# A graph layer with residual and layer norm: 68 copied columns per engine and octet, register loads of eight, sums in two PSUM banks, and the product of x and W1b made three and copied two octets ahead

## The chip, the core and the metric

The kernel runs on one core of a Trainium2 chip. The core has five engines with a stream of instructions each: TensorE (PE in the profile; PEld is its weight load), VectorE (DVE), ScalarE (ACT), GpSimd (POOL) and SyncE (SP), which here only issues transfers and loads registers. The metric is the device time of one execution in microseconds (us), less is better. Before the change the median of three runs is 5184.74 us (5167.56 to 5185.11).

## What is computed

There are 12500 nodes with 64 features each and 400000 edges, sorted by their target node.

```python
def _L0_gnn_ref(x, edge_index, edge_attr, W1, b1, W2, b2, W3, b3):
    src, dst = (edge_index[0], edge_index[1])
    m_in = jnp.concatenate([x[src], x[dst], edge_attr], axis=-1)
    h = jax.nn.silu(m_in @ W1 + b1)
    messages = jax.nn.silu(h @ W2 + b2)
    agg = jax.ops.segment_sum(messages, dst, num_segments=x.shape[0])
    node_in = jnp.concatenate([x, agg], axis=-1)
    return jax.nn.silu(node_in @ W3 + b3)
...
x = _layernorm(x + _L0_gnn_ref(...), axis=-1)
```

W1 has three blocks of rows: W1a for x[src] (64 rows), W1b for x[dst] (64 rows) and one for the edge attributes (16 rows).

## The kernel before

**Tiles and octets.** The edges are cut into 3125 tiles of 128. Eight tiles are an octet; 391 octets are the turns of the main loop, which is unrolled (line 601 and on). Since the edges are sorted by target, all targets of an octet lie in a window of 48 nodes.

**The first layer of an octet** (`first_layer`, line 434) has two shares. The share of the targets and the attributes is one matmul, line 441, with weights `xw`: 96 rows of x W1b for the window, twice over and masked, and 32 rows of attribute weights. The 96 rows are made for every octet: SyncE fetches the window's 48 columns of x (`window_load`, line 392), TensorE multiplies them by W1b (`window_product`, line 397) into a PSUM tile named `mm`, and VectorE copies that with the mask into one of three `xw` tiles (`window_copy`, line 402). The share of the sources comes in one of three ways, and pairs of tiles (256 edges) are handed out to them:

- GpSimd gathers rows of x W1a, made in advance, from memory: one indirect transfer per tile of 128 edges (`gather`, line 373), three octets ahead, into five buffers `ga`. TensorE turns and adds them at line 454.
- VectorE and ScalarE copy columns of x, which stays in on-chip memory transposed (`xs`), one instruction per edge, into a tile `cx` of 128 columns with two edges each (`columns`, lines 297 and 299). Where a column lies comes from a register, loaded beforehand from the list of source indices (line 290, a register load of up to 16 or 8 values). Per octet VectorE copies 32 + 32 columns and ScalarE 32 + 28 (`VCOLS`, `ACOLS`). A `cx` tile that is full takes the place of two gathers; TensorE multiplies it by W1a at line 451. The index list of a tile is fetched by SyncE (`index`, line 351) and scaled to addresses by VectorE (`address`, line 359).
- SyncE fetches 16 single rows per octet (`rows`, line 324), which makes a pair every 16 octets.

The first 12 octets (`RAW`) gather raw rows of x and multiply them by W1a themselves (lines 443 to 449), while the tables of x W1a are made (`table`, line 175).

**The rest of an octet.** ScalarE applies silu (line 458, `h`), TensorE multiplies by W2 (`second_layer`, lines 467 and 469), ScalarE applies silu again (line 473, `m`). `add_up` (line 482) sums the messages per node with 8 matmuls against a 0/1 matrix `eh`, into one quarter of a PSUM tile, `pg`, with four quarters used by turns. `add_window` (line 487) adds that to the sums of all nodes, on VectorE. VectorE makes the 0/1 matrices by comparing (`compare_dst`, line 424, and `compare_nodes`, line 430). Every four tiles of nodes that are complete get their second part (lines 499 to 552).

**The order.** TensorE, ScalarE, VectorE and SyncE run their instructions in the order in which the loop issues them (line 598); waits between engines are put in by the framework, and a tile is overwritten only when those who read its earlier content are done. In turn o the streams are:

- SyncE: index list for o+3, now and then other loads, the window of o+3, 16 rows.
- TensorE: product for o+1, first layer of o, sums of o-2, second layer of o-1.
- VectorE: add of o-4, comparison of targets for o+1, 32 columns, window copy for o+1, comparison of nodes for o+1, 32 columns, addresses for o+2.
- ScalarE: 32 columns, h of o, 28 columns, m of o-1.

**PSUM.** There are eight banks: two for `mm` (pool `mis`: products, raw tiles, tables, node products), one for `wrow`, two for `p1` (first layer), two for `p2` (second layer), one for `pg` (the sums).

Of the kernel before, what the change touches and what calls it, by code (L numbers as in the profile page):

```python
# [27 lines left out]
AHEAD = 3  # L28
RAW = 12
TABLES = 7  # L30
ACOLS = (32, 28)
VCOLS = (32, 32)
ROWS = 16
LOADS = (16, 8)
XBASE = (0, 64 << 18)
XADDR = 36864
LAG = CT * P // 32
# [60 lines left out]
def windows(ctx, tc, ident, badi, pa, x, xt, src_c, src_row, dst_c, dst_row, attr_t, dst_2, attr_2, base, w1, b1, w2, b2, w3, b3, out, edges):  # L98
# [70 lines left out]
    zero = const.tile([P, 1], F32, name="zero")  # L169
    nc.vector.memset(zero, 0.0)  # L170

    mis = ctx.enter_context(tc.tile_pool(name="mis", bufs=2, space=PSUM))


    def table(c):
        n = min(8 * P, N - c)
        ps = mis.tile([P, 8, D], F32, name="mm")
        k = (n + P - 1) // P
        for i in range(k):
            o = c + i * P  # L180
            nc.tensor.matmul(ps[:, i, :], xs[0:D, o:o + P], w1ab[:, 0, :], start=True, stop=True)
        j = c // (8 * P) % RB
        t = v[:, 2 * j:2 * j + 2].rearrange("p a i d -> p (a i) d")
        nc.scalar.copy(t[:, :k], ps[:, :k])
        f = n // P
        if f:
            nc.scalar.dma_start(pa[c:c + f * P, :].rearrange("(i p) d -> p i d", p=P), t[:, :f])
        if n % P:
            nc.scalar.dma_start(pa[c + f * P:c + n, :], t[:n % P, f, :])
# [43 lines left out]
    w1bb = fast.tile([D, 2, D], F32, name="w1bb")  # L233
    nc.vector.tensor_copy(w1bb, w1ab[:, 1:2, :].to_broadcast([D, 2, D]))
    xw = []
    for k in range(3):
        t = fast.tile([P, P], F32, name=f"xw{k}")
        nc.vector.memset(t, 0.0)
        for q in range(2):
            nc.sync.dma_start(t[E + q * A:E + (q + 1) * A, q * D:(q + 1) * D], w1[2 * D:2 * D + A, :])  # L240
        xw.append(t)
# [6 lines left out]
    with tc.tile_pool(name="gat", bufs=AHEAD + 2) as gat, tc.tile_pool(name="drp", bufs=2) as drp, \  # L248
# [2 lines left out]
            tc.tile_pool(name="work", bufs=2) as work, tc.tile_pool(name="win", bufs=3) as win, \  # L251
            tc.tile_pool(name="ps1", bufs=2, space=PSUM) as ps1, \
            tc.tile_pool(name="ps2", bufs=2, space=PSUM) as ps2, \
            tc.tile_pool(name="psa", bufs=1, space=PSUM) as psa, \
            tc.tile_pool(name="cx", bufs=4) as cx, tc.tile_pool(name="cxi", bufs=3) as cxi, \
            tc.tile_pool(name="rx", bufs=2) as rx, tc.tile_pool(name="rxi", bufs=2) as rxi, \
            tc.tile_pool(name="nx", bufs=2) as nx, tc.tile_pool(name="nv", bufs=1) as nv:
# [10 lines left out]
        cols, indices = {}, {}  # L268
        xb = xs.bitcast(U8)

        def columns(o, eng, part):
            if o < RAW:
                return
            lo = (o - RAW) * RATE
            if eng == ENG.Activation:
                lo, n = lo + sum(ACOLS[:part]), ACOLS[part]
            else:
                lo, n = lo + sum(ACOLS) + sum(VCOLS[:part]), VCOLS[part]
            hi, todo = lo + n, n
            while lo < hi:  # L280
                j, e0 = lo // (2 * P), lo % (2 * P)
                if j >= len(pairs):
                    return
                n = min(hi - lo, P - e0 % P, LOADS[lo > hi - todo])
                if pairs[j] not in cols:
                    cols[pairs[j]] = cx.tile([P, P], F32, name="cx")
                t = cols[pairs[j]].bitcast(U8)
                s = e0 // P
                h = slice(s * D, (s + 1) * D)
                _, regs = nc.values_load_multi_w_load_instructions(  # L290
                    indices[j][0:1, e0:e0 + n], engines=(eng,), min_val=XBASE[s] + XADDR,
                    max_val=XBASE[s] + XADDR + 4 * (N - 1), skip_runtime_bounds_check_because="src names a node")
                for e, r in zip(range(e0 % P, e0 % P + n), regs):
                    to, frm = t[h, 4 * e:4 * e + 4], xb[h, ds(r - (XBASE[s] + XADDR), 4)]
                    if eng == ENG.DVE:

                        nc.vector.tensor_reduce(to, frm[:, :, None], AX.X, OP.max)  # L297
                    else:
                        nc.scalar.copy(to, frm)  # L299
                lo += n  # L300


        rpairs = []
# [55 lines left out]
                    nc.vector.tensor_scalar(t[:, h], t[:, h], 4.0, float(XBASE[s] + XADDR), op0=OP.mult, op1=OP.add)  # L359

        winrow, winreg = {}, {}
        sums = psa.tile([P, 4, S], F32, name="pg")

        def gather(o):
            c, t0, n, first, last = octs[o]
# [29 lines left out]
        def window_product(o):  # L395
            pw = mis.tile([P, P], F32, name="mm")
            nc.tensor.matmul(pw[:E, :], winrow[o].rearrange("k s w -> k (s w)"), w1bb.rearrange("k s m -> k (s m)"),  # L397
                             start=True, stop=True)
            winrow[o] = pw

        def window_copy(o):
            nc.vector.tensor_tensor(xw[o % 3][:E, :], winrow.pop(o)[:E, :], mask[:E, :], op=OP.mult)  # L402

        def load(c, o0=0, o1=CT // OT):

# [28 lines left out]
        def first_layer(o):  # L434
            c, t0, n, first, last = octs[o]
            n2 = n + n % 2
            k = n2 // 2
            ga = got.pop(o)
            oh, eh = hots.pop(o)
            p1 = ps1.tile([P, OT // 2, P], F32, name="p1")  # L440
            nc.tensor.matmul(p1[:, :k], xw[o % 3], oh, start=True, stop=False, skip_group_check=True)  # L441
            if o < RAW:
                pt = mis.tile([P, OT // 2, P], F32, name="mm")
                for i in range(k):
                    nc.tensor.matmul(pt[:, i, :], ga[:, 2 * i:2 * i + 2, :].rearrange("p s d -> p (s d)"), ident,  # L445
                                     start=True, stop=True)
                xg = work.tile([P, OT // 2, P], F32, name="m")
                nc.vector.tensor_copy(xg[:, :k], pt[:, :k])
                nc.tensor.matmul(p1[:, :k], w1d, xg[:, :k], start=False, stop=True, skip_group_check=True)
            if o in pairs:  # L450
                nc.tensor.matmul(p1[:, 0, :], w1d, cols.pop(o), start=False, stop=False, skip_group_check=True)  # L451
            for i in range(1 if o in pairs else 0, k if o >= RAW else 0):
                g2 = single.pop(o) if o in rpairs and i == 1 else ga[:, 2 * i:2 * i + 2, :]
                nc.tensor.matmul(p1[:, i, :], g2.rearrange("p s d -> p (s d)"), ident,  # L454
                                 start=False, stop=(i == k - 1), skip_group_check=True)
            columns(o, ENG.Activation, 0)
            h = work.tile([P, OT // 2, P], F32, name="h")
            nc.scalar.activation(h[:, :k], p1[:, :k], AF.Silu, bias=b1s)  # L458
            made[o] = h, eh
# [16 lines left out]
        def add_up(o):  # L476
            c, t0, n, first, last = octs[o]
            m, eh = made.pop(o)
            pg = sums[:, o % 4, :]
            for i in range(n):  # L480
                s = i % 2
                nc.tensor.matmul(pg[s * D:(s + 1) * D, :], m[:, i, :], eh[:, i, :],  # L482
                                 start=(i < 2), stop=(i >= n - 2), skip_group_check=True)

        def add_window(o):
            a = agg[:, ds(winreg.pop((ENG.DVE, o)), S)]
            nc.vector.tensor_tensor(a, a, sums[:, o % 4, :], op=OP.add)  # L487


        groups = [(c, min(G * P, N - c)) for c in range(0, N, G * P)]  # L490
# [16 lines left out]
        def node_product(q):  # L507
            c, n = groups[q]
            p = n // G
            assert p * G == n  # L510
            po = mis.tile([P, G, D], F32, name="mm")
            av = agg[:, c:c + n].rearrange("k (p i) -> k i p", i=G)
            xv = xs[0:D, c:c + n].rearrange("k (p i) -> k i p", i=G)
            nc.tensor.matmul(po[:p], ones[:, :p], b3r, start=True, stop=False, skip_group_check=True)
            for i in range(G):
                nc.tensor.matmul(po[:p, i, :], xv[:, i], w3x, start=False, stop=False, skip_group_check=True)  # L516
                nc.tensor.matmul(po[:p, i, :], av[:, i], w3s, start=False, stop=(i == G - 1), skip_group_check=True)  # L517
            nodes[q].append(po)
# [62 lines left out]

        for o in range(min(AHEAD, NO)):
            gather(o)
        window_load(0)
        window_product(0)
        window_copy(0)
        load(0, 0, 1)
        load(0, 1, 3)
        window_load(1)
        window_load(2)  # L590
        relative(0, CT)
        lims = nv.tile([P, 2, LP], F32, name="lims")
        tables = list(range(0, N, 8 * P))
# [4 lines left out]
        with tc.manual_schedule(engines={ENG.PE, ENG.Activation, ENG.DVE, ENG.SP}):  # L598
            compare_dst(0)
            compare_nodes(0)  # L600
            for o in range(NO + 1):
# [27 lines left out]
                    gather(o + AHEAD)  # L629
                if o + 2 < NO and octs[o + 2][3] and o + 2:  # L630
                    load(octs[o + 2][0])
                if o + 3 < NO:
                    window_load(o + 3)
                if o + 1 < NO:
                    window_product(o + 1)
                if o % 4 == 2:
                    bases(ENG.DVE, o - 2)
                if o >= 4:
                    add_window(o - 4)
                if o + 1 < NO:  # L640
                    compare_dst(o + 1)
                columns(o, ENG.DVE, 0)
# [1 line left out]
                    first_layer(o)  # L644
                if o == 0:
                    nc.vector.tensor_copy(b2r, b2p[:, None, :].to_broadcast([3, OT, D]))
                if o + 1 < NO:
                    window_copy(o + 1)
                    compare_nodes(o + 1)
                columns(o, ENG.DVE, 1)  # L650
                if o == 1:
# [12 lines left out]
                    add_up(o - 2)  # L664
                if o >= 1:
                    second_layer(o - 1)
                address(o + 2)
                raddress(o + 2)
                rows(o)
# [21 lines left out]
        nc.vector.tensor_copy(badi, bs)  # L691

        add_up(NO - 1)
        for o in range(NO - 3, NO):
            add_window(o)
        for f, a in todo.get(NO, []):
            f(*a)
# [267 lines left out]
```

## Time and profile before

| what | value |
|---|---|
| median of three runs | 5184.74 us |
| the profiled execution | 5200.1 us |
| its span, first to last instruction | 5197.9 us |
| instructions | 107486 |
| granted clock of TensorE | 0.629 |
| gathers from the table on GpSimd (line 373) | 2619, of 0.944 us each |
| row fetches on SyncE (line 324) | 5888 |
| register loads of line 290 on VectorE | 2391, of 0.340 to 1.340 us |
| register loads of line 290 on ScalarE | 2352, of 0.305 to 1.255 us |
| line 424 and line 430 on VectorE | 0.674 and 0.545 us each |
| line 458 and line 473 on ScalarE | 0.684 and 0.593 us each |

The profile is one execution, recorded by the hardware. In its rows "DVE cx L297" is a group of instructions of VectorE at line 297 that write the tile cx; "busy" is time in which at least one of them ran, the mean is that of a single one, and "idle before" is the time in which the engine ran nothing just before them, with what ended it. "Issue" there stands for time in which the engine waited for nothing that the profile shows. Register loads, branches and the issue of transfers do not count as busy. The views in order of time give the start, the length, the engine and the line, and merge neighbours of one kind (x8: eight of them).

### The profile page before, as it was taken

What the parts mean: (1) busy time and instruction counts of PE and PEld (TensorE: products, weight loads), DVE (VectorE), ACT (ScalarE), POOL (GpSimd) and SP (SyncE); (2) the same over time, 40 slices, a digit from 0 to 9 for tenths busy, and PEclk for the clock granted to TensorE, in tenths of its full rate; (3) what the DMA queues carried; (4) which work ended last, traced back from release to release, by engine and by line L of the source; (5) the groups of instructions that cost most, each with busy time, mean ns of one, the idle gap of its engine ahead of it and who ended that gap; (6) DMA issues with size and microseconds to landing.
All of it is one profiled execution on the core that took longest, in us unless ns stands there. A gap on an engine that the chain in (4) does not pass through costs nothing. (4 is left out here: it accounts for less than half of the span.)

```text
span 5197.9 us, 107486 instructions
## 1 busy us (share of the span) xinstructions
PE 2932.5 (56%) x15131; PEld 2075.4 (40%) x15131; DVE 2641.3 (51%) x26395; ACT 2906.1 (56%) x23402; POOL 2565.3 (49%) x2724
## 2 busy tenths in 40 slices
PE   5655655555555555555564655656555555555566
PEld 3443434434433344343343434434433343344344
DVE  1255555545555555555555555555555555555555
ACT  1255555555555655655556565555556555655555
POOL 5544454454444544445444444545454444555453
PEclk7666565666666666666656566565656666665656
DMA  4321111211211121122112211211211221121121
GB/s 85 86 46 39 40 39 40 47 39 40 46 42 43 40 46 40 40 43 42 41 40 49 43 40 42 44 39 40 47 40 40 44 47 40 40 47 39 40 46 40
DMA packets 203943, 229.98 MB, mean 44 GB/s; under 512 B 133612, under 2 KB 141988, under 8 KB 202324
## 3 DMA queue, kind: packets, MB, share of 16 engines
q1 hardware_dynamic: 101528, 122.61, 10.5%
q0 software_dynamic: 86880, 89.14, 9.1%
q10 hardware_dynamic: 14812, 11.26, 0.9%
q14 instruction: 595, 4.87, 0.3%
q8 instruction: 128, 2.10, 0.2%
HBM read 216.36 MB, written 6.40 MB: 43 GB/s over the span
## 5 line engine op out<-in xcount | busy, mean ns | idle before, releaser
L373 POOL DMA_INDIRECT ga<-pa,sc x2619 | 2472.2, 944 | 2516.1 <-PE p L454 1699.8
L299 ACT COPY cx<-xs 64x4 uint8 x22560 | 2404.2, 188 | 1406.1 <-issue 1362.4
L297 DVE TENSOR_REDUCE cx<-xs 64x4 uint8 x24032 | 1910.3, 150 | 1806.6 <-issue 1740.9
L441 PE MATMUL p<-oh,xw 128*128 128x512 f32 (+1 forms) x782 | 772.4, 1089 | 1529.3 <-DVE xw L402 727.6
L441 PEld LDWEIGHTS p<-oh,xw 128*128 128x128 f32 x782 | 187.1, 297 | 1637.1 <-DVE xw L402 776.3
L482 PE MATMUL pg<-eh,m 128*64 128x48 f32 x6250 | 363.0, 277 | 588.6 <-ACT m L473 174.1
L454 PEld LDWEIGHTS p<-ident,ga 128*128 128x128 f32 x2620 | 591.3, 314 | 194.9 <-issue 193.6
L469 PE MATMUL p<-w2d,h 128*128 128x128 f32 x3126 | 642.0, 369 | 1.5 <-issue 1.4
L469 PEld LDWEIGHTS p<-w2d,h 128*128 128x128 f32 x3126 | 545.3, 263 | 133.0 <-issue 133.0
L454 PE MATMUL p<-ident,ga 128*128 128x128 f32 x2620 | 593.2, 397 | 0.0
L482 PEld LDWEIGHTS pg<-eh,m 128*64 128x64 f32 x6250 | 312.1, 189 | 680.2 <-issue 342.2
L473 ACT ACTIVATE m<-p 128x512 f32<-128x512 f32 x391 | 231.8, 593 | 474.9 <-remote 308.9
L458 ACT ACTIVATE h<-p,b1s 128x512 f32<-128x512 f32 x391 | 267.4, 684 | 319.0 <-remote 138.6
L402 DVE TENSOR_TENSOR xw<-mm,mask 96x128 f32<-96x128 f32 x391 | 110.4, 282 | 439.9 <-issue 392.4
L397 PE MATMUL mm<-w1bb,xr 64*96 64x128 f32 x782 | 241.0, 401 | 72.6 <-ACT z L523 49.9
L424 DVE TENSOR_TENSOR oh<-dr,wrow 96x512 f32<-96x512 int32 x391 | 263.6, 674 | 6.3 <-issue 3.5
L430 DVE TENSOR_TENSOR eh<-wrow,dc 128x384 f32<-128x384 f32 x391 | 213.2, 545 | 42.2 <-issue 42.2
L467 PE MATMUL p<-b2r,one 3*128 3x512 bf16 x391 | 194.5, 498 | 0.0
L451 PEld LDWEIGHTS p<-cx,w1d 128*128 128x128 f32 x364 | 116.0, 319 | 175.4 <-issue 175.4
L397 PEld LDWEIGHTS mm<-w1bb,xr 64*96 64x96 f32 x782 | 127.8, 214 | 144.7 <-issue 68.7
L487 DVE TENSOR_TENSOR agg<-agg,pg 128x48 f32 x391 | 77.3, 198 | 123.4 <-remote 32.3
L373 POOL DMA_INDIRECT ga<-in_x,sc x96 | 91.0, 948 | 63.5 <-PE mm L445 28.9
(81 smaller groups left out, 802.7 us busy)
## 6 DMA issues: line engine op xcount, KB each, us to landing
rx<-pa SPq DMA_DIRECT2D x5888, 0.2 KB
dr<-in_dst SPq DMA_DIRECT2D x260, 288.0 KB
ga<-pa,sc POOLq DMA_INDIRECT x2619
oh<-in_attr SPq DMA_DIRECT2D x130, 192.0 KB
xr<-in_xt SPq DMA_DIRECT2D x391, 24.0 KB
xs<-in_xt ACTq DMA_DIRECT2D x12, 512.0 KB
pa<-v ACTq DMA_DIRECT2D x12, 256.0 KB
xa<-in_x SPq DMA_DIRECT2D x24, 128.0 KB
```

Of the source, the lines that this page charges most:

```text
L297: nc.vector.tensor_reduce(to, frm[:, :, None], AX.X, OP.max)
L299: nc.scalar.copy(to, frm)
L373: nc.gpsimd.indirect_dma_start(out=ga[:, i, :], out_offset=None, in_=x if o < RAW else pa[:, :], in_offset=bass.IndirectOffsetOnAxis(ap=sc ...
L397: nc.tensor.matmul(pw[:E, :], winrow[o].rearrange("k s w -> k (s w)"), w1bb.rearrange("k s m -> k (s m)"), start=True, stop=True)
L424: nc.vector.tensor_tensor(oh[:E, :], dr[:, e:e + w], wn[:E, o:o + 1].to_broadcast([E, w]), op=OP.is_equal)
L430: nc.vector.tensor_tensor(eh[:, :n], row[:, None, :].to_broadcast([P, n, S]), rel[:, t0:t0 + n, None].to_broadcast([P, n, S]), op=OP.is_equal)
L441: nc.tensor.matmul(p1[:, :k], xw[o % 3], oh, start=True, stop=False, skip_group_check=True)
L454: nc.tensor.matmul(p1[:, i, :], g2.rearrange("p s d -> p (s d)"), ident, start=False, stop=(i == k - 1), skip_group_check=True)
L458: nc.scalar.activation(h[:, :k], p1[:, :k], AF.Silu, bias=b1s)
L469: nc.tensor.matmul(p2[:, 2 * i:2 * i + 2, :].rearrange("p s d -> p (s d)"), h[:, i, :], w2d, start=False, stop=(i == k - 1), skip_group_ch ...
L473: nc.scalar.activation(m[:, :n2], p2[:, :n2], AF.Silu)
L482: nc.tensor.matmul(pg[s * D:(s + 1) * D, :], m[:, i, :], eh[:, i, :], start=(i < 2), stop=(i >= n - 2), skip_group_check=True)
```

## The change

- `ACOLS` goes from (32, 28) to (36, 32) and `VCOLS` from (32, 32) to (36, 32): 68 columns per octet on each of the two engines, 136 in all where there were 124.
- `LOADS` goes from (16, 8) to 8: a part of columns was loaded as sixteen registers first and eights after; now in eights only. `columns` is split into `pieces`, `addresses` and itself; its instructions are otherwise the same.
- `pg`: instead of one tile with four quarters in one bank, a tile of its own for each octet, in two banks by turns. The add of a window comes three octets after, not four.
- `mm` gets one bank instead of two. Tables and node products use `p2`, the raw tiles of the first 12 octets use `p1`.
- Four `xw` tiles instead of three. In turn o the window of o+4 is fetched (before: o+3), the product is made for o+3 and at the end of TensorE's turn (before: o+1, at its beginning), and VectorE copies that of o+2 (before: o+1), at the same place in its turn.
- VectorE's registers for the windows (line 382) are loaded one turn earlier of every four.

```diff
-ACOLS = (32, 28)
-VCOLS = (32, 32)
+ACOLS = (36, 32)
+VCOLS = (36, 32)
 ROWS = 16
-LOADS = (16, 8)
+LOADS = 8
...
-    mis = ctx.enter_context(tc.tile_pool(name="mis", bufs=2, space=PSUM))
+    mis = ctx.enter_context(tc.tile_pool(name="mis", bufs=1, space=PSUM))
...
-        ps = mis.tile([P, 8, D], F32, name="mm")
+        ps = ps2.tile([P, OT, D], F32, name="p2")
...
-    for k in range(3):
+    for k in range(4):
         t = fast.tile([P, P], F32, name=f"xw{k}")
...
-            tc.tile_pool(name="psa", bufs=1, space=PSUM) as psa, \
+            tc.tile_pool(name="psa", bufs=2, space=PSUM) as psa, \
...
-                n = min(hi - lo, P - e0 % P, LOADS[lo > hi - todo])
+                n = min(hi - lo, P - e0 % P, LOADS)
+                yield j, e0, n
+                lo += n
...
+        def addresses(eng, j, e0, n):
+            s = e0 // P
+            _, regs = nc.values_load_multi_w_load_instructions(
+                indices[j][0:1, e0:e0 + n], engines=(eng,), min_val=XBASE[s] + XADDR,
+                max_val=XBASE[s] + XADDR + 4 * (N - 1), skip_runtime_bounds_check_because="src names a node")
+            return regs
+
+        def columns(o, eng, part):
+            for j, e0, n in pieces(o, eng, part):
+                regs = addresses(eng, j, e0, n)
...
-        sums = psa.tile([P, 4, S], F32, name="pg")
+        sums = {}
...
-            nc.vector.tensor_tensor(xw[o % 3][:E, :], winrow.pop(o)[:E, :], mask[:E, :], op=OP.mult)
+            nc.vector.tensor_tensor(xw[o % 4][:E, :], winrow.pop(o)[:E, :], mask[:E, :], op=OP.mult)
...
-                pt = mis.tile([P, OT // 2, P], F32, name="mm")
+                pt = ps1.tile([P, OT // 2, P], F32, name="p1")
...
-            pg = sums[:, o % 4, :]
+            pg = sums[o] = psa.tile([P, S], F32, name="pg")
...
-            nc.vector.tensor_tensor(a, a, sums[:, o % 4, :], op=OP.add)
+            nc.vector.tensor_tensor(a, a, sums.pop(o), op=OP.add)
...
-            po = mis.tile([P, G, D], F32, name="mm")
+            po = ps2.tile([P, OT, D], F32, name="p2")[:, :G]
...
-                if o + 3 < NO:
-                    window_load(o + 3)
-                if o + 1 < NO:
-                    window_product(o + 1)
-                if o % 4 == 2:
-                    bases(ENG.DVE, o - 2)
-                if o >= 4:
-                    add_window(o - 4)
+                if o + 4 < NO:
+                    window_load(o + 4)
+                if o % 4 == 1:
+                    bases(ENG.DVE, o - 1)
+                if o >= 3:
+                    add_window(o - 3)
...
+                if o + 2 < NO:
+                    window_copy(o + 2)
                 if o + 1 < NO:
-                    window_copy(o + 1)
                     compare_nodes(o + 1)
...
                     second_layer(o - 1)
+                if o + 3 < NO:
+                    window_product(o + 3)
```

Ahead of the loop four windows are fetched, three products made and two copied (before: three, one and one); after it, two adds are left instead of three.

More of the change, by code (lines that the diff above doesn't have):

```diff
@@ L269, in windows, with pieces @@
         xb = xs.bitcast(U8)
-        def columns(o, eng, part):
+        def pieces(o, eng, part):
             if o < RAW:
@@ L278, in columns @@
                 lo, n = lo + sum(ACOLS) + sum(VCOLS[:part]), VCOLS[part]
-            hi, todo = lo + n, n
+            hi = lo + n
             while lo < hi:
@@ L289, in columns @@
                 h = slice(s * D, (s + 1) * D)
-                _, regs = nc.values_load_multi_w_load_instructions(
-                    indices[j][0:1, e0:e0 + n], engines=(eng,), min_val=XBASE[s] + XADDR,
-                    max_val=XBASE[s] + XADDR + 4 * (N - 1), skip_runtime_bounds_check_because="src names a node")
                 for e, r in zip(range(e0 % P, e0 % P + n), regs):
@@ L299, in columns @@
                         nc.scalar.copy(to, frm)
-                lo += n
         rpairs = []
@@ L440, in first_layer @@
             p1 = ps1.tile([P, OT // 2, P], F32, name="p1")
-            nc.tensor.matmul(p1[:, :k], xw[o % 3], oh, start=True, stop=False, skip_group_check=True)
+            nc.tensor.matmul(p1[:, :k], xw[o % 4], oh, start=True, stop=False, skip_group_check=True)
             if o < RAW:
-                pt = mis.tile([P, OT // 2, P], F32, name="mm")
+                pt = ps1.tile([P, OT // 2, P], F32, name="p1")
                 for i in range(k):
@@ L583, in windows @@
             gather(o)
-        window_load(0)
-        window_product(0)
-        window_copy(0)
+        for o in range(4):
+            window_load(o)
+        for o in range(2):
+            window_product(o)
+            window_copy(o)
+        window_product(2)
         load(0, 0, 1)
         load(0, 1, 3)
-        window_load(1)
-        window_load(2)
         relative(0, CT)
@@ L693, in windows @@
         add_up(NO - 1)
-        for o in range(NO - 3, NO):
+        for o in range(NO - 2, NO):
             add_window(o)
```

## The prediction

> **What bounds the kernel now.** I read the busy times first, then the groups, then single octets in order of time, and last the waits. An octet is one turn of the main loop; 391 of them fill the 5197.9 us span, and from the 30th to the 380th the period is 13.19 us (distance between the add of one window, line 487, and the next).
>
> ```profile
> PE 2932.5 (56%) x15131; PEld 2075.4 (40%) x15131; DVE 2641.3 (51%) x26395; ACT 2906.1 (56%) x23402; POOL 2565.3 (49%) x2724
> ...
> L299 ACT COPY cx<-xs 64x4 uint8 x22560 | 2404.2, 188 | 1406.1 <-issue 1362.4
> L297 DVE TENSOR_REDUCE cx<-xs 64x4 uint8 x24032 | 1910.3, 150 | 1806.6 <-issue 1740.9
> ```
>
> No engine looks full: all stand near half. But the idle time of the two engines that copy columns is nearly all "issue", which is no wait for another engine's result. VectorE's stream in order of time shows what it is:
>
> ```profile
> 2610.69 0.62 DVE L297 TENSOR_REDUCE cx<-xs 64x4 uint8 x8 [0.30 <-issue]
> 2611.35 0.21 DVE L487 TENSOR_TENSOR agg<-agg,pg 128x48 f32 x1
> 2611.47 0.68 DVE L424 TENSOR_TENSOR oh<-dr,wrow 96x512 f32<-96x512 int32 x1
> 2612.36 1.78 DVE L297 TENSOR_REDUCE cx<-xs 64x4 uint8 x24 [0.21 <-issue]
> ...
> 2616.02 0.40 DVE L297 TENSOR_REDUCE cx<-xs 64x4 uint8 x5 [0.24 <-issue]
> 2616.70 0.21 DVE L297 TENSOR_REDUCE cx<-xs 64x4 uint8 x2 [0.28 <-issue]
> 2617.44 0.15 DVE L297 TENSOR_REDUCE cx<-xs 64x4 uint8 x1 [0.53 <-issue]
> 2618.16 0.15 DVE L297 TENSOR_REDUCE cx<-xs 64x4 uint8 x1 [0.57 <-issue]
> ```
>
> Columns start 0.0635 us apart (five in 0.40 us, one of them 0.15), until a register load (line 290) steps in: the x8 group follows a gap of 0.30 us. From 2616.7 on something else rules: one column per 0.71 us. SyncE's row fetches (line 324) are held at the same time:
>
> ```profile
> 2609.80 1.19 SPq L324 DMA_DIRECT2D rx<-pa  x4
> ...
> 2614.90 10.13 SPq L324 DMA_DIRECT2D rx<-pa  x14
> ```
>
> Four in 1.19 us before, fourteen in 10.13 us here. I call these held stretches. They lie where GpSimd's gathers are in flight while SyncE issues rows; ScalarE's columns are held too:
>
> ```profile
> 2608.50:2611.00 2.50, 2.50 (x7) 1.47 (x7) 2.18 (x30) 2.48 (x23) 0.00 (x0) 0.50 0.00 1
> 2616.50:2623.50 7.00, 3.78 (x10) 2.46 (x10) 1.38 (x11) 1.04 (x6) 4.56 (x5) 0.68 0.16 30
> ```
>
> (Stages; after the length, busy time and count of PE, PEld, DVE, ACT, POOL.) Without gathers VectorE ran 30 instructions in 2.5 us; beside five gathers, 11 in 7 us. Marking every gap of 0.5 to 1.7 us between SyncE's row instructions as held, from 300 to 5100 us, gives 2216 us of 4800 (46%). Outside them VectorE was busy 1935 of 2584 us, had a register load running in 414 more, and stood with neither for only 235. ScalarE: busy 2112, neither 334. TensorE: neither 645.
>
> Last, the waits around line 402, the copy of x W1b, and line 482, the sums:
>
> ```profile
> L402 DVE TENSOR_TENSOR xw<-mm,mask x391: 269/287/289, 13.7 to 5166.9; 96x128 f32<-96x128 f32 x196
> ...
>   PE mm L397: 3.8, 3
> ...
>   PEld p L441: 776.3, 161
> ```
>
> ```profile
> L482 PE MATMUL pg<-eh,m x6250: 222/307/343, 97.2 to 5179.0; 128*64 128x48 f32 x196
> ...
>   DVE agg L487: 168.1, 110
> ```
>
> VectorE waited 3.8 us in all for the product; TensorE waits for VectorE, at line 441 and, with line 482, for the window's add. So **the pace is VectorE's own stream plus the held stretches**, ScalarE close behind; TensorE, and GpSimd, which waits 1699.8 us for TensorE to free its buffers, follow.
>
> A check on that reading: over stretches of six octets I fitted the period to the gathers and to VectorE's extra work in them (node statistics, divisions, address arithmetic). A gather goes with 0.78 us (error 0.09), a microsecond of extra VectorE work with 0.53 us (0.13), of extra ScalarE work with 0.5 (0.4).
>
> **The change part by part.**
>
> *Columns on VectorE.* 64 become 68 per octet. Applying the slicing to all octets: 24032 become 25444, +1412 at 0.0635 us = +90 us.
>
> *Loads of eight on VectorE.* The two parts were sliced 16+8+8, now 8+8+8+8+4 and 8+8+8+8; with the cuts at tile borders 2391 loads become 3368. An eight-register load between columns sets them 0.47 us apart (0.30 idle; median of 763 spacings 0.47) where 0.06 is normal: price 0.40. There are 765 more of these: +306. A four-register load makes a spacing of 0.22 (106 cases): 0.16 each, 214 more: +34. The first load of a part runs beside the compare ahead of it (0.68 and 0.54 us) and sticks out when it has sixteen registers (1.10 us): by 0.21 and 0.24 in the rows above. With eight (0.597 us) it is covered: 682 times 0.22 = -150. That saving is 0 at least, and 0.50 each at most (1.10 - 0.597), -344; I take the rows' own gap. Seventeen more index tiles bring two address operations each of 0.2 us: +7. Sum +287 us, between 93 and 437.
>
> Some of it falls into held stretches, where the pace is set otherwise: 17% of the columns started there. 83% of 287 is 238 (77 to 363).
>
> A rule speaks more sharply against the loads: the Trainium skill, "DMA: Bandwidth & Descriptors", section on latency and other measured facts, gives register loads from memory a floor of about 600 ns. By it the 977 more loads would cost an estimated 586 us whatever their size. The trace disagrees on the floor (340 ns for four registers).
>
> *Columns on ScalarE.* 60 become 68, +2940 at 0.0935 us (32 in 3.09 us in one unbroken row) = +275 us. Its eight-register loads take 0.547 us while eight columns take 0.75, and its columns run on through them (68 of some 1200 broke the rhythm); so the finer loads cost nothing. If that cover went, the extra load time (1506 to 1762 us) would be +256. ScalarE's 334 free microseconds (362 over the span) take most of the 275; what comes through, I count below.
>
> *Gathers.* Pairs of tiles served by columns go from 182 to 199, so 34 gathers fewer. At 0.78 us each, -27 us; at GpSimd's own spacing of 1.25 us, -43; at least 0.
>
> *Product three ahead, copy two ahead, four xw.* No instruction is added per octet: product, window fetch and copy keep their counts and move by an octet. On TensorE the product is now last of its turn, behind the second layer. With one "mm" buffer instead of two, the product for o+3 must wait for line 402's copy for o+2, and line 441 of the next octet is queued behind it, then adding up, second layer and ScalarE's h. So line 441 still starts after that copy, now 0.74 us later (the two matmuls of line 397). 195 of 391 octets start line 441 within 0.4 us of the copy: 144 us at most if TensorE set the end. I take 0: it hides behind TensorE's 645 free microseconds, and nothing VectorE waits for came out of TensorE late (half of its copies start 16 us after their product). SyncE's window fetch one octet earlier moves past nothing: row fetches and index loads keep their order behind it; its buffer is freed by a product which TensorE now ends at the same place in its stream.
>
> *Sums in two banks.* The 168.1 us that line 482 waited for line 487 go; what is late next is ScalarE's m (446.9 us in the same view). On VectorE the add moves one octet closer to its sum. The sum it now needs followed m by some 1.1 us, and m(o-3) ended 7 to 18 us before the octet began. Worth 0; at best those 168, at worst the 123.4 us that line 487 has idle before it now, once more.
>
> *Node and table products in p2, the raw tiles in p1.* The 49.9 us that line 397 waited for the node sigmoid go, TensorE's again: 0. The first twelve octets take two p1 buffers each: at worst the 101.1 us of idle time ahead of line 448's twelve copies doubles; I take 0, since the tables no longer share a buffer with them.
>
> **Sum.** VectorE's path in full: +238 - 27 = +211 us. The fit gives nearly the same another way: 0.53 of 287 and 0.3 of 275 (between 0 and the fitted 0.5), less 27: +208. The profiled execution took 5200.1 us (2.2 us around its span), 15 above the median of 5184.74, so **5395 us** for the median. Its own range, from the bounds 77 to 363 of VectorE and 27 for the gathers, is 5235 to 5520.
>
> **Rivals.**
>
> *Held stretches shrink.* TensorE ends its turn earlier where line 482 waited, frees GpSimd's buffers sooner, and gathers slide into the 4.4 us per octet in which SyncE issues no rows (1.93 from the last row to the window fetch, 2.47 from there to the next row). VectorE is busy 26% of a held stretch, so each held microsecond saved gives 0.74. The stretches fill about 2400 us of the span; a fifth less gives -355 us: 5040. It beats the added work from 12% on. For it: the overlap is a matter of phase, and octets differ by 2.5 us in it (one standard deviation). Against: line 441 still hangs on the copy, rows are as many, gathers 1% fewer.
>
> *Held stretches grow.* VectorE falls behind SyncE, whose rows then come earlier into the gathers: octets in which SyncE's window fetch came before VectorE's turn began were held 7.3 to 8.4 us, those where it came 3 us after, 4.0. A tenth more is +178 us: 5573. Against: SyncE has hardly any free time to run ahead.
>
> *Nothing comes through.* VectorE's 235 idle microseconds outside (255 over the span) absorb the 238, and the gathers' 27 remain: 5185 - 27 + 15 = about 5175. Against: a passed share of 0.53 in the fit. That the columns don't move at all can't be: the lists set them.
>
> **How the numbers follow.** Forecast 55%, growth 14%, nothing 10%, shrinking 21%. Within 0.5% (5159 to 5211), which is about what this kernel's runs can tell from no change, lie 7 in 100; faster 21, the shrinking; the rest, 72, slower. Leaving out the far half of the shrinking and of the growth, 8 times in 10 the time lies in 5130 to 5560.
>
> **What would show it.** Right: some 3370 loads at line 290's successor on VectorE, an 8-column rhythm with 0.30 us gaps, the gaps after lines 424 and 430 gone, period near 13.7 us, held share still 44 to 48%, VectorE hardly waiting for TensorE. ScalarE's free time should nearly vanish, line 441's wait for the copy stay as a wait of line 397. Wrong: a held share that moves by more than 4 points, a period below 13.2, or VectorE idle for a sum or a product.

## The result and the profile after

The median after is 5481.01 us (5470.35 to 5491.54, four runs) against 5184.92 us for the kernel before beside it (5167.56 to 5191.62, four runs): a ratio of 1.0576, 95% interval 1.0543 to 1.0609. The change makes the kernel slower by 296 us; the forecast was 211 us slower.

Line numbers have moved: columns are 307 (VectorE) and 309 (ScalarE), the comparisons 433 and 439, the window copy 411, the product 406, gathers 382, row fetches 333, sums 491, the add of a window 496. First the busy times and the groups of the page after, as shown of before:

```profile
PE 2888.0 (53%) x15131; PEld 2033.1 (37%) x15131; DVE 2793.3 (51%) x27842; ACT 3226.0 (59%) x26342; POOL 2532.0 (46%) x2690
...
L382 POOL DMA_INDIRECT ga<-pa,sc x2585 | 2439.1, 944 | 2836.2 <-PE p L463 2034.4
L309 ACT COPY cx<-xs 64x4 uint8 x25500 | 2734.7, 188 | 1540.5 <-issue 1493.6
L307 DVE TENSOR_REDUCE cx<-xs 64x4 uint8 x25444 | 2073.3, 148 | 1886.7 <-issue 1801.0
L406 PE MATMUL mm<-w1bb,xr 64*96 64x128 f32 x782 | 277.5, 455 | 2050.0 <-DVE xw L411 1278.5
```

The counts are those that the working used: 25444 columns on VectorE (+1412), 25500 on ScalarE (+2940), 34 gathers fewer. TensorE did not get slower and was not asked for more; GpSimd stands idle 320 us longer (2836.2 for 2516.1), since its waits for TensorE to free its buffers grew by 335 (2034.4 for 1699.8). Those two follow. The wait for the window copy, which was line 441's (727.6 of the 1529.3 us that TensorE's matmuls stood idle before it), is now line 406's (1278.5 of 2050.0).

VectorE in order of time, some 24 us of the kernel after (start, length, engine and line, count, idle time before):

```profile
3010.97 0.67 DVE L433 TENSOR_TENSOR oh<-dr,wrow 96x512 f32<-96x512 int32 x1
3011.66 0.62 DVE L307 TENSOR_REDUCE cx<-xs 64x4 uint8 x8
3012.57 0.62 DVE L307 TENSOR_REDUCE cx<-xs 64x4 uint8 x8 [0.30 <-issue]
3013.49 0.62 DVE L307 TENSOR_REDUCE cx<-xs 64x4 uint8 x8 [0.30 <-issue]
...
3028.41 0.15 DVE L307 TENSOR_REDUCE cx<-xs 64x4 uint8 x1 [0.57 <-issue]
3029.12 0.15 DVE L307 TENSOR_REDUCE cx<-xs 64x4 uint8 x1 [0.56 <-issue]
3029.83 0.21 DVE L307 TENSOR_REDUCE cx<-xs 64x4 uint8 x2 [0.56 <-issue]
```

The gap behind the comparison of line 433 is gone, and columns come in eights with 0.30 us between: the loads of eight, as worked out. Lower down is a held stretch, one column per 0.71 us as before. SyncE shows the same in its row fetches, free and held:

```profile
3009.96 0.87 SPq L333 DMA_DIRECT2D rx<-pa  x3
...
3025.89 10.42 SPq L333 DMA_DIRECT2D rx<-pa  x16
```

With the prediction's own measure (a gap of 0.5 to 1.7 us between SyncE's row instructions is held), octets 30 to 380, in us per octet. "Neither" is time outside the held stretches in which the engine neither ran an instruction nor had a register load running (a load is counted to 0.1 us after its end); these last two rows are means from 300 us to 100 us before the end, so their sums differ a little from the row above them.

| | before | after |
|---|---|---|
| period | 13.19 | 13.96 |
| held | 6.15 | 6.65 |
| outside | 7.04 | 7.31 |
| VectorE outside: busy / load / neither | 5.32 / 1.14 / 0.64 | 5.41 / 1.25 / 0.74 |
| ScalarE outside: busy / load / neither | 5.81 / 0.38 / 0.91 | 6.33 / 0.13 / 0.94 |

0.77 us more over 379 octets is 292 us, nearly the whole loss of 296: it is spread evenly over the loop. Of it 0.50 us lies in the held stretches and 0.27 outside; the held share hardly moved (46.2% to 47.0%).

A last view, SyncE's queue: what its index fetch (line 351, now 360) waited for, before, then after (total us, times, longest).

```profile
SPq L351 <- ACTq L290: 17.1, 17, 9.6
SPq L351 <- DVEq L290: 3.5, 1, 3.5
```

```profile
SPq L360 <- ACTq L290: 123.1, 52, 9.1
SPq L360 <- DVEq L290: 106.5, 30, 11.8
```

SyncE can fetch a new index list only when the register loads of an older one are done. It now waits 230 us for the two engines that load registers, where it waited 21: those two are the ones that fell behind.

### The profile page after: what moved, and what is told of

Read it like the earlier page. It is cut to its first block, busy times and chain, and to the rows that moved or that the text cites. A ratio compares the mean times of both kernels' runs of the same rounds, so it can differ in the third digit from the quotient of the medians.

```text
span 5477.8 us, 114041 instructions
## 1 busy us (share of the span) xinstructions
PE 2888.0 (53%) x15131; PEld 2033.1 (37%) x15131; DVE 2793.3 (51%) x27842; ACT 3226.0 (59%) x26342; POOL 2532.0 (46%) x2690
## 5 line engine op out<-in xcount | busy, mean ns | idle before, releaser
L382 POOL DMA_INDIRECT ga<-pa,sc x2585 | 2439.1, 944 | 2836.2 <-PE p L463 2034.4
L309 ACT COPY cx<-xs 64x4 uint8 x25500 | 2734.7, 188 | 1540.5 <-issue 1493.6
L307 DVE TENSOR_REDUCE cx<-xs 64x4 uint8 x25444 | 2073.3, 148 | 1886.7 <-issue 1801.0
L406 PE MATMUL mm<-w1bb,xr 64*96 64x128 f32 x782 | 277.5, 455 | 2050.0 <-DVE xw L411 1278.5
L406 PEld LDWEIGHTS mm<-w1bb,xr 64*96 64x96 f32 x782 | 147.2, 245 | 2139.9 <-DVE xw L411 1332.1
L463 PEld LDWEIGHTS p<-ident,ga 128*128 128x128 f32 x2586 | 569.5, 309 | 174.0 <-issue 170.1
L478 PE MATMUL p<-w2d,h 128*128 128x128 f32 x3126 | 600.0, 351 | 0.0
L463 PE MATMUL p<-ident,ga 128*128 128x128 f32 x2586 | 571.2, 390 | 0.0
L478 PEld LDWEIGHTS p<-w2d,h 128*128 128x128 f32 x3126 | 508.2, 247 | 128.8 <-issue 128.8
L460 PE MATMUL p<-cx,w1d 128*128 128x128 f32 x398 | 121.7, 408 | 0.0
```

Source lines behind the costliest of these rows:

```text
L382: nc.gpsimd.indirect_dma_start(out=ga[:, i, :], out_offset=None, in_=x if o < RAW else pa[:, :], in_offset=bass.IndirectOffsetOnAxis(ap=sc ...
L478: nc.tensor.matmul(p2[:, 2 * i:2 * i + 2, :].rearrange("p s d -> p (s d)"), h[:, i, :], w2d, start=False, stop=(i == k - 1), skip_group_ch ...
```

## The experiments

Twelve runs were made, on five chips, and the chips fell into two kinds. On those numbered 10 and 5, as in the comparison above, the kernel before took 5190 to 5250 us and has the held stretches. On those numbered 13, 4 and 14 the same kernel took 3429 to 3441 us, and the traces taken there have no such stretches. This was not foreseen, and it decided what each run could tell. The times below stand beside the kernel before on the same chip.

### What the chips without held stretches showed

Three single parts and the kernel before without rows ran first, on chip 13.

```diff
-LOADS = (16, 8)
+LOADS = (8, 8)
```

> The kernel before with register loads of eight from the start of a part; the columns stay at 64 and 60. Theory (VectorE's stream sets the pace): some 680 more interior loads of eight at 0.40 us on VectorE, less 682 first loads that stop sticking out (0.22 each), 83% outside held stretches: +100 us, ratio 1.02. Rival (the loads are hidden by the held stretches): no change, ratio 1.00. Rival (the loads carry the whole loss): ratio 1.05.

```diff
-ACOLS = (32, 28)
-VCOLS = (32, 32)
+ACOLS = (36, 32)
+VCOLS = (36, 32)
```

> The kernel before with 68 columns on each engine, loads still 16 first and 8 after, nothing else changed. Theory: VectorE +90 us of columns and +56 of four-register loads, ScalarE +275 of which a third comes through, 34 gathers fewer -27: +150 to +200 us, ratio 1.03 to 1.04. Rival (the loss comes from the moved product and its single mm buffer): 0 to +50 us, ratio 1.00 to 1.01. Rival (fewer gathers pay): ratio 0.99.

The third has everything of the change but the columns and the loads of eight: four xw tiles, the product three and the copy two octets ahead, sums in two banks, products in p2, raw tiles in p1.

```diff
+                if o + 2 < NO:
+                    window_copy(o + 2)
...
+                if o + 3 < NO:
+                    window_product(o + 3)
...
+            pg = sums[o] = psa.tile([P, S], F32, name="pg")
```

> The kernel after with the columns and loads of before: only the PSUM banks, the four xw and the moved product, copy and adds. Theory: 0 us, between -50 and +50, ratio 0.99 to 1.01. Rival (line 450 starts 0.74 us later and TensorE's delay reaches the end): +144 us, ratio 1.03. Rival (the freed waits help): ratio below 0.99.

The fourth fetches no single rows; the tiles that these served are gathered.

```diff
-ROWS = 16
+ROWS = 0
...
-        while True:
+        while ROWS:
```

> The kernel before without SyncE's single rows; their 23 pairs of tiles are gathered by GpSimd. Theory of the prediction (held stretches are gathers and row fetches at the same time): the held stretches all but vanish, VectorE's period falls towards its clear time, ratio 0.7 or below. Rival (the gathers alone hold the engines): held time stays, 46 more gathers at 0.78 us give +36 us, ratio 1.00 to 1.01.

| | time, us | ratio to before, 95% |
|---|---|---|
| the kernel before | 3434.39 | |
| loads of eight | 3438.20 | 1.0011 (1.0000 to 1.0022) |
| 68 columns | 3446.60 | 1.0040 (1.0022 to 1.0058) |
| order and banks | 3440.03 | 1.0014 (1.0000 to 1.0029) |
| no rows | 3489.96 | 1.0165 (1.0146 to 1.0184) |

The theory's times were worked out for a kernel with held stretches, and but for the 0 of the order none of them came. What took the place of the held stretches is in the first run's trace. GpSimd in order of time:

```profile
1703.89 0.94 POOL L373 DMA_INDIRECT ga<-pa,sc  x1 [0.30 <-issue]
1705.13 0.94 POOL L373 DMA_INDIRECT ga<-pa,sc  x1 [0.30 <-issue]
```

SyncE and VectorE beside these gathers:

```profile
1703.74 5.10 SPq L324 DMA_DIRECT2D rx<-pa  x16
```

```profile
1706.34 1.32 DVE L297 TENSOR_REDUCE cx<-xs 64x4 uint8 x16
1707.96 0.62 DVE L297 TENSOR_REDUCE cx<-xs 64x4 uint8 x8 [0.30 <-issue]
```

Sixteen rows take 5.10 us in the midst of gathers, and VectorE keeps its rhythm. GpSimd is what never rests: gathers follow each other 1.249 us apart, and 2619 of them are 3271 us of a span of 3431. The row fetches are worth having here because they replace gathers: the run without them has 46 gathers more, 57 us at that spacing, and took 56 us longer. Columns do not pay the other way round: the run with 68 of them has 34 gathers fewer, 42 us at that spacing, but in its trace GpSimd waits 54.0 us for TensorE to free its buffers (10.7 in the run with loads of eight), and its gathers take as long from the first to the last, 3274 us for 3275.

Four more tried the columns from the other side.

```diff
-ACOLS = (32, 28)
-VCOLS = (32, 32)
+ACOLS = (16, 16)
+VCOLS = (16, 16)
```

> The kernel before with 16 + 16 columns on each engine, 64 per octet instead of 124; GpSimd gathers 7.4 tiles per octet instead of 6.9. Theory (held stretches come from gathers in flight, and between them VectorE's and ScalarE's columns set the pace): with held stretches the columns fit almost wholly into them, the period falls from 13.2 us to GpSimd's own 7.4 x 1.25 = 9.2 to 10 us, ratio 0.72 to 0.80. Where GpSimd gathers without a pause already, 9.2 instead of 8.7 us, ratio 1.06. Rival (each gather costs the path 0.78 us or more, columns are worth their time): ratio above 1.02 with held stretches.

It met chip 4, again without held stretches: 3651.43 for 3432.15 us, 1.0640 (1.0622 to 1.0658). It gathers 176 tiles more; at 1.249 us that is 220 us, and 219 were measured. On such a chip the gathers set the pace; what fewer columns give on a held one, this run could not say. Beside it ran the order again, and more columns on one engine each:

> The kernel after with the columns and loads of before, again, for a chip with held stretches. Theory of the prediction: 0, ratio 0.99 to 1.01 there. Rival (the product behind the copy in a single mm buffer delays TensorE, and with it GpSimd's buffers and ScalarE): +50 us and more, ratio 1.01 to 1.03.

```diff
-VCOLS = (32, 32)
+VCOLS = (36, 32)
```

> The kernel before with 68 columns on VectorE alone (ScalarE stays at 60, loads 16 first and 8 after). Theory: +90 us of columns, +56 of four-register loads, 83% of it clear, 11 gathers fewer: +100 to +120 us with held stretches, ratio 1.02; none without them. Rival (ScalarE is the pacer): ratio 1.00.

```diff
-ACOLS = (32, 28)
+ACOLS = (36, 32)
```

> The kernel before with 68 columns on ScalarE alone (VectorE stays at 64, loads 16 first and 8 after). Theory: 275 us of columns, most of it in ScalarE's free time, 23 gathers fewer: +30 to +90 us with held stretches, ratio 1.005 to 1.02. Rival (ScalarE is the pacer): the whole 275, ratio 1.05.

| | time, us | ratio to before, 95% |
|---|---|---|
| order and banks, once more | 3439.98 | 1.0022 (1.0007 to 1.0038) |
| 68 columns on VectorE alone | 3450.43 | 1.0053 (1.0036 to 1.0070) |
| 68 columns on ScalarE alone | 3427.96 | 0.9987 (0.9976 to 0.9998) |

More columns on VectorE cost 0.53%, on ScalarE they save 0.13%, and both together cost the 0.40% of the second run. That VectorE's stream is what the columns lengthen here is not shown by it: with the columns on VectorE alone the gathers take 3269 us from the first to the last, 6 us less than in the run with loads of eight, and the loss lies behind the last of them (54 us to the end of the span, for 32). All parts of the change sum to under 1% on these chips. By that sum the 5.8% belong to the held stretches.

### What the held chips showed

On chip 10 the whole change was measured again, and beside it the columns and the loads of eight in before's order and banks.

> The kernel after, unchanged, beside the kernel before on one chip. The four experiments so far ran on a chip where the kernel before takes 3434 us, without held stretches and with GpSimd gathering without a pause. Theory (the 5.8% come from work added to engines that the held stretches keep short of time): where held stretches are in the profile, ratio 1.05 to 1.06; where GpSimd gathers without a pause, 34 gathers fewer at 1.249 us are -42 us and the three parts measured so far (+0.1%, +0.4%, +0.1%) come to a ratio of 1.00 to 1.01. Rival (the change is slow on every chip by the same share): 1.058 on both kinds.

```diff
-ACOLS = (32, 28)
-VCOLS = (32, 32)
+ACOLS = (36, 32)
+VCOLS = (36, 32)
 ROWS = 16
-LOADS = (16, 8)
+LOADS = (8, 8)
```

> The kernel before with 68 columns on each engine and loads of eight; PSUM banks and order as before. Theory: with held stretches this is nearly the whole loss, ratio 1.04 to 1.06; without them 1.00 to 1.01. Rival (the order and the single mm buffer carry the loss): below 1.02 with held stretches.

| | time, us | ratio to before (5197.58 us), 95% |
|---|---|---|
| the whole change | 5478.86 | 1.0532 (1.0464 to 1.0599) |
| columns and loads alone | 5431.38 | 1.0433 (1.0365 to 1.0500) |

Columns and loads alone cost 234 us. The order and the banks add the rest: the four runs of the whole change (5456.48 to 5491.64) all lie above the four without the new order (5419.66 to 5445.89), with means 44 us apart (standard error 10, so about 20 to 69).

The accounting per octet shows that the two parts do not act alike:

| | before | columns and loads | the whole change, two profiles |
|---|---|---|---|
| period | 13.19 | 13.83 | 13.96, 13.89 |
| held share, by SyncE's row gaps | 46.2% | 52.4% | 47.0%, 47.0% |
| held, by row gaps | 6.15 | 7.32 | 6.65, 6.61 |
| held, by gaps on SyncE, VectorE or ScalarE | 6.98 | 7.50 | 7.27, 7.12 |
| VectorE outside (row gaps): neither | 0.64 | 0.30 | 0.74, 0.73 |
| ScalarE outside (row gaps): neither | 0.91 | 0.42 | 0.94, 0.89 |
| first row fetch, after the turn's first add | 2.27 | 1.42 | 2.05, 1.99 |

With columns and loads alone both engines lose about half of their free time, and rows move 0.85 us earlier in VectorE's turn: the held part grows, by 0.5 to 1.2 us per octet according to the measure. That the earlier rows are the reason is not shown; both measures see a hold only while an engine has instructions to start, so engines with more work also show more of it. The new order takes about half of that growth off again, but gives both engines back their idle time, and ends 0.1 us per octet worse.

The next kernel goes through six stages in one execution, in before's order, each with its own columns, loads and rows; with no row fetches after octet 320.

```diff
+STAGES = [(12, (32, 28), (32, 32), (16, 8)), (74, (36, 32), (36, 32), (16, 8)), (136, (32, 28), (32, 32), (8, 8)),
+          (198, (36, 32), (36, 32), (8, 8)), (260, (16, 16), (16, 16), (16, 8)), (322, (32, 28), (32, 32), (16, 8))]
+ROWEND = 320
...
+            ACOLS, VCOLS, LOADS = stage(o)
+            lo = starts[o]
```

> The kernel before with six stages in one execution, so that they meet the same chip: octets 12 to 73 as before; 74 to 135 with 68 columns on each engine, loads 16 and 8; 136 to 197 columns as before, loads of eight only; 198 to 259 both; 260 to 321 16 + 16 columns on each engine; 322 to 385 columns as before and no row fetches. Periods by stage in us, with held stretches: theory 13.2, 13.6, 13.45, 13.85, 9.2 to 10, 13.2 to 13.4 (gathers alone hold the engines). Rivals: 13.2 in the third stage (loads hidden); above 13.4 in the fifth (a gather costs more than the columns it saves); below 9 in the sixth (row fetches are needed for a hold). Without held stretches, theory: GpSimd's 1.249 us times the gathers, 8.6 to 8.9 in all stages but the fifth, 9.3 there.

It met chip 5, with held stretches (5179.61 us, the kernel before beside it 5197.14, one run each). Period of each stage, with the standard error over its octets:

| stage | period, us |
|---|---|
| as before | 13.14 ± 0.23 |
| 68 columns | 13.40 ± 0.19 |
| loads of eight | 13.30 ± 0.23 |
| both | 13.64 ± 0.21 |
| 16 + 16 columns on each engine | 13.03 ± 0.89 |
| as before, no rows | 12.63 ± 0.31 |

The first four agree with the working but do not prove it: the steps are 0.26 and 0.16 us, together 0.50 (0.64 in the run above), each with an error of 0.3. The fifth contradicts the reading. I had expected 9.2 to 10 us from halving the columns; VectorE and ScalarE did become idle, and the period stayed, as far as its error of 0.89 us tells. Busy time of the engines in the "both" stage and in this one (length of the window; busy time and count of PE, PEld, DVE, ACT, POOL):

```profile
2768.00:3518.00 750.00, 409.90 (x2089) 289.13 (x2089) 401.63 (x4066) 465.13 (x3861) 356.00 (x376) 0.62 0.19 41
3596.00:4312.00 716.00, 403.45 (x2094) 284.75 (x2093) 232.64 (x2071) 255.58 (x1876) 385.67 (x408) 0.62 0.22 45
```

The waits of the fifth stage:

```profile
DVE oh L435 <- DMA dr<-in_dst: 222.3, 15, 20.6
...
PEld mm L408 <- DMA xr<-in_xt: 82.1, 17, 9.8
```

SyncE's own waits there, the two longest:

```profile
SPq L403 <- remote: 21.1, 2, 10.7
SPq L333 <- DMA rx<-pa: 12.6, 23, 1.4
```

VectorE fell from 401.63 to 232.64 us of work and now waits 222.3 us for a list that SyncE fetches late, TensorE for its window. SyncE, whose row fetches are held too, waits 46 us in all of these 716, and 19 of the 723 in the first stage: its stream was full before too, and it became the pace when VectorE was relieved. A part of the period is the gathers' own: there are 7.4 of them per octet here, 6.9 in the first stage, and what each adds to the held time was not taken apart.

The sixth stage (12.63 us, a little under the 13.2 to 13.4 expected) takes SyncE's load away instead. SyncE then waits for the two engines' register loads, about half of 720 us:

```profile
SPq L362 <- DVEq L299: 193.7, 16, 18.0
SPq L362 <- ACTq L299: 158.1, 14, 22.4
```

So VectorE and ScalarE set the pace there. The stage also tells what a held stretch needs. VectorE, and GpSimd over the same time:

```profile
4703.51 1.70 DVE L306 TENSOR_REDUCE cx<-xs 64x4 uint8 x23 [0.31 <-issue]
4705.89 0.21 DVE L306 TENSOR_REDUCE cx<-xs 64x4 uint8 x2 [0.68 <-issue]
4706.62 0.15 DVE L306 TENSOR_REDUCE cx<-xs 64x4 uint8 x1 [0.52 <-issue]
4707.33 0.21 DVE L306 TENSOR_REDUCE cx<-xs 64x4 uint8 x2 [0.56 <-issue]
...
4713.03 1.46 DVE L306 TENSOR_REDUCE cx<-xs 64x4 uint8 x21 [0.49 <-issue]
```

```profile
4701.64 0.94 POOL L384 DMA_INDIRECT ga<-pa,sc  x1 [1.91 <-remote]
...
4710.39 0.95 POOL L384 DMA_INDIRECT ga<-pa,sc  x1 [0.30 <-issue]
```

SyncE issued no row here. The stretch begins some 4 us after the first gather of the burst started and ends 1.7 us after the last one ended: the engines are held beside gathers without any row fetch.

The last kernel was to relieve SyncE and the two engines at once: in the new order, few columns without row fetches.

```diff
+STAGES = [(12, (32, 28), (32, 32), (16, 8)), (140, (16, 16), (16, 16), (16, 8)), (222, (24, 24), (24, 24), (16, 8)),
+          (304, (32, 28), (32, 32), (16, 8))]
+ROWEND = 142
```

> The kernel after (its order and banks) with four stages in one execution: octets 12 to 139 columns and loads of before, with row fetches; 140 to 221 16 + 16 columns on each engine and no row fetches; 222 to 303 24 + 24 on each and none; 304 to 385 columns of before and none. Theory now (with held stretches SyncE's row fetches and the two engines' columns share the pace, so that neither alone can be taken away with gain): periods 13.2 to 13.4, 9.4 to 10, 9.5 to 11, 12.6 us with held stretches. Rival (each gather in flight costs the path its 1.25 us and more): above 12 in the second stage. Rival (the order of after costs a part of the loss): above 13.4 in the first. Without held stretches GpSimd's 1.249 us times the gathers: 8.7, 9.4, 9.1, 8.8.

It met chip 14, without held stretches (3544.61 us, before 3430.67). Its periods were 8.63, 9.41, 9.05 and 8.82 us, with 6.91, 7.53, 7.24 and 7.07 gathers per octet: 1.249 us times the gathers and nothing more, close to the 8.7, 9.4, 9.1 and 8.8 expected for such a chip. So the question it was made for stays open.

## Why the prediction was right, and where it was not

**The pace.** "VectorE's own stream plus the held stretches" was right in the direction that the change took: more work there lengthens the turn, SyncE now waits for the register loads, TensorE's and GpSimd's waits only grow. It was not the whole: SyncE's stream is as full, and half of the columns less bring nothing that shows (13.03 ± 0.89 for 13.14). That the held stretches need row fetches beside the gathers was wrong; the run without rows has them too, at 12.63 us per octet.

**Columns and loads: 211 us.** 238 on VectorE, less 27 for the gathers. Alone they measured 234 (1.0365 to 1.0500 of 5197.58 us is 190 to 260). The counts were exact: 3368 loads, a spacing of 0.47 us across one of eight (median of 1701 cases) and 0.22 across one of four (303 cases). How much of the 234 each part carries is not resolved (0.26 and 0.16 us per octet, with errors of 0.3). The floor that the Trainium skill gives for a register load ("DMA: Bandwidth & Descriptors", latency and other measured facts) does not hold here: a load of four registers took 340 ns on VectorE, and all loads there took 1735 us before and 1915 after, 180 more for 977 more loads, where 600 ns each would have made 586. That the sum of 211 fits the 234 so well is partly luck. The working put the added time outside the held stretches, with the stretches as long as before; in the run with these two parts alone VectorE's time outside is shorter (5.17 busy and 1.12 loading per octet, for 5.32 and 1.14) and the held time longer. The total followed the work, its place did not.

**ScalarE's free time.** "Should nearly vanish" came half true with columns and loads alone (0.91 to 0.42 us per octet), and not at all with the new order (0.94). Its register loads ran beside its columns as taken: time in a load outside the held stretches fell from 0.38 to 0.13 us per octet.

**The order: 0, at most 144.** This is the term that was wrong. Product three ahead, one "mm" bank, sums in two banks and the products in p2 were each costed at nothing, since TensorE has free time; together they cost 44 us (20 to 69) beside the columns on a held chip, and 0.14% and 0.22% of 3434 us, 5 to 8 us, on the others, where the first interval begins at no cost at all. The forecast's wait did move as described, from line 441 to line 406, and VectorE waited 0.9 us for a product, as far as the profile names what it waited for. But the cover was not free for all: in the new order ScalarE's h starts 5.60 us into VectorE's turn, for 1.59 with columns and loads alone (and 4.38 in the kernel before), and VectorE and ScalarE are idle outside the held stretches 0.44 and 0.52 us per octet more, about as long as before the change. That the one causes the other is not shown, nor which of the moved pieces does it, and the order without the columns did not run on a held chip.

**Two banks.** The sums' wait for the window's add is gone, and what is late next is ScalarE's m, as said. In the view of line 491, what TensorE waited for before it (us, times; weight loads and matmuls counted each):

```profile
  ACT m L482: 697.1, 240
```

It was 446.9 us before.

**The rivals.** *Growth* was given 5573 us and 14 in 100. Earlier rows and a longer held time, as it described, are what the columns and loads show by themselves (52.4% held, the mark for "wrong" being four points); in the whole change the held time grew by 8% (6.15 to 6.65), close to the tenth that it took. The 5481 us lie as near to its 5573 as to the forecast's 5395. *Shrinking* named a relieved TensorE; the new order did take 0.67 us of held time per octet off, by the row gaps, and no time was won by it: both engines then stood idle elsewhere. *Nothing* is ruled out. The held share in the mark of 44 to 48% is therefore two opposite moves that cancel, and no proof of the mechanism that the forecast named.

**The sum.** Columns and loads were 23 us short and the order 44; the remaining 20 or so lie within what chips and runs differ by (the kernel before is at 5184.92 us on one held chip and 5197.58 on another).

Left open: what few columns without row fetches give on a held chip; the gathers' own price there; and the whole change on a chip without held stretches, which was not run (its parts sum to under 1%). No kernel tried is shown to be faster than both on a held chip.

## What to carry to other kernels

When no engine is full and the idle time is "issue", lay the engines' streams beside each other in time before naming the bound: here three engines slow down together, and relieving one of them only hands the pace to the next. Cost added instructions by their spacing to the next instruction, register loads between them included, and trust the total more than the place where it is to appear. A reordering that only moves work into another engine's free time can still shift the phase of what waits for it, and deserves a price with a sign of its own.

## What the runs showed of the hardware

**Chips differ.** One program, 5197.9 us in the profiled span on one chip, takes 3434 us on another. On the slower kind, while GpSimd's indirect gathers are in flight, SyncE, VectorE and ScalarE each start one instruction per 0.71 us, and the granted clock of TensorE is 0.62 to 0.64; on the other kind there is no such stretch, and the clock of the same program is 0.77 to 0.78. Why, the runs do not tell; the clock may be a result of the pace as well as a cause.

**The stretches need no row fetches.** They are there in the stage without rows (12.63 us per octet). In the kernel before, by the wider of the two measures, a burst of six gathers comes with 5.71 us held and one of eight with 8.51, so 1.4 us for each more.

**A gather's spacing.** 1.249 us from one to the next on GpSimd wherever buffers are free, 0.94 us of it busy; on chips without held stretches it alone gives the time of the runs with fewer columns and without rows to within 2 us.
